# One silu for both streams, the second half first, and the loads of the opening in another order

## The chip, the cores and the metric

The program runs on one core of a Trainium2 chip. The metric is the device time of one execution in microseconds, the median over a few runs. A core has five engines with a queue of instructions each, which meet through semaphores: TensorE (PE, matrix products, with its weight loads shown as PEld), VectorE (DVE), ScalarE (ACT), GpSimd (POOL) and SyncE (SP, which here issues the DMAs). Each engine runs its queue in order, so an instruction that waits holds up everything behind it on that engine.

## The reference

The input is four images of 128 channels and 96 x 96 points. They are normalised by groups, run as a sequence in four directions (rows, rows backwards, columns, columns backwards) through one block, fused, and added to the input. The block, cut to what matters:

```python
def _scan1d(x, ...):                                # x: (16, 128, 9216), four directions of four images
    t = _grouped1x1(x, in_proj_w, in_proj_b, G)     # 4 groups, 128 -> 512 channels
    u, gate = t[:, :HID], t[:, HID:]                # HID = 256
    u = jax.nn.silu(u)
    u = depthwise_conv(u, dw_w)                     # 5 taps along the sequence
    s = _conv1x1(u, ssm_in_w)                       # 32 channels
    a = clip(DMIN + (DMAX - DMIN) * sigmoid(_conv1x1(u, ssm_delta_w, ssm_delta_b)))
    bb, cc = tanh(_conv1x1(u, ssm_b_w, ssm_b_b)), tanh(_conv1x1(u, ssm_c_w, ssm_c_b))
    hst = scan(a, bb * s)                           # h = a * h + bb * s
    u = u + _conv1x1(cc * hst + ssm_d * s, ssm_out_w)
    u = _grouped1x1(u * sigmoid(gate), mix_w, mix_b, G)
    return _conv1x1(u, out_proj_w, out_proj_b)

y = concat of the four directions, put back in place
return x + einsum('oc,bchw->bohw', fuse_w, y) + fuse_b      # the block is fed group_norm(x)
```

## The kernel before

The work of the body is cut into steps (16 lines of an image, for two directions at once) and each step into four phases `p` of the sequence, which are taken in the order `TURN = (1, 2, 3, 0)`. Position n of the sequence lies in phase n mod 4. One phase of both directions is a pair; `pair(t)` is written for the first six, `pair_on(t)` for the rest, and `tail()` ends. The two directions of a step are called the streams, `s` = 0 and 1. They lie in different partitions of the input tiles `x_in[0]` and `x_in[1]`: stream `s` in partitions 64s to 64s+63 as front rows, and the other 64 partitions hold the rows for the gate (`load_gate`).

A front is the part up to the silu. The 256 channels are two halves `j`. `in_proj(step, g, s, j, bank)` multiplies one row block of `x_in[s]` with the normalised weights `wn` in four 32 x 32 products (two passes each, so eight records in a trace). For `j` = 0 the index `g` is a group of channels and all four phases come out together; for `j` = 1 `g` is a phase. `silu` adds the bias `bnorm` and writes 385 columns of the tile `sil`; `silu_both` exists for the same over two neighbouring banks. `edges` zeroes a border column. Then the first half goes through a convolution on PE (`conv` and `conv_less`, products with the diagonal tiles `band` and `less`; each needs all four groups of the first half) and is copied to `u`. The second half goes through five taps on DVE (`taps`, lines 824 and 828). Tap k of a pair with phase p reads phase (p + k) mod 4, so the first pair (p = 1) reads the phases 1, 2, 3, 0, 1 in turn. From the second pair on the first tap is on ACT (line 826). The taps of all pairs use the same two PSUM banks, 0 and 1, so that a pair's first tap waits for the last tap of the pair before it. `proj` multiplies `u` for the scan; in the first pair it has the next step's first front between its products.

The opening is `start()`. While the first image arrives in ten pieces (`load_x`, 24 blocks), DVE takes its statistics block by block (`bn_stats`, line 330). `stats_first` then makes of them, in pieces that are released by `next(pieces)`, the group means (product with `mv`), the spreads (product with `ex`), the standard deviation, the scaled weights `wn` (line 206) and the bias `bnorm` (lines 216, 217). Between the pieces PE runs fillers, products that nobody reads. In the same place stand the fused weights: `outer(d)` multiplies the output weights with the fuse weights (line 1296, one direction `d` after the other, each emptied from PSUM by a copy), `inner` multiplies the mix weights with these (line 1304), and DVE writes them to `w_fin`, which is needed only by the last products of a pair. The order of all instructions is the order in which the program is written (a manual schedule); a wait stands wherever a tile demands it.

All loads of the opening but one are issued by SP, in the order of the program: `x`, `fuse`, `main` (the projection weights, read by line 206 and by POOL at line 398), the two front blocks, and the gates. Eight semaphores are shared among the DMAs in turn. SP therefore issues a DMA only when the one eight before it has landed.

## Time and profile before

| | us |
|---|---|
| median of 3 runs | 1717.79 |
| lowest and highest run | 1713.65, 1720.6 |
| the profiled execution | 1714.65 |
| its span on the core | 1712.9 |
| PE busy, share of the span | 1691.0, 99% |
| DVE, ACT, POOL busy | 1505.1, 1495.4, 1481.7 |
| last statistics block ends | 18.4 |
| first silu starts | 23.82 |
| last silu of the opening ends | 32.36 |

The profiled execution's own time stands beside the span of its trace; the 1.75 us between them lie around the trace. Times of the profile count from the span's start. A busy PE is not a PE at its peak, because the ends of products are modelled and overlap. In rows of the timeline an operation can be shown with its count, and in brackets stands how long its engine was idle before it and what ended that.

### The profile page before, as it was taken

The page shows a single profiled execution, that of the slowest core. Times are in us where ns is not written, and L with a number is a line of the kernel's source. Part 1 is how long each engine was busy: PE and PEld are TensorE (multiplying, and loading weights), DVE is VectorE, ACT ScalarE, POOL GpSimd, SP SyncE. Part 2 cuts the span into 40 slices and gives each one's busy share as a digit, 9 for nine tenths or more (in the row PEclk, how much of TensorE's full clock was granted, in tenths as well). Part 3 has the DMA queues.
Part 4 walks back from the last instruction along what each step waited for, and adds up shares of the span by engine and source line. Part 5 has one row for each costly group of instructions (what it writes and reads, how often), then busy time and mean ns, then how long its engine had stood idle before and what let it go on. Part 6 is the DMA issues. An engine that isn't in the chain of part 4 may idle for free.

```text
span 1712.9 us, 49914 instructions
## 1 busy us (share of the span) xinstructions
PE 1691.0 (99%) x20410; PEld 663.9 (39%) x20410; DVE 1505.1 (88%) x1506; ACT 1495.4 (87%) x2435; POOL 1481.7 (87%) x1455
## 2 busy tenths in 40 slices
PE   7999999999999999999999999999999999999998
PEld 3333333333333333333333333333333333333333
DVE  6899999888789999888888999988888888888897
ACT  4789999889889899888998898988998898988875
POOL 3689999888789999988888989999888889998887
PEclk9999999999999999999999999999999999999999
DMA  7855884468994788437897488633799538853365
GB/s 240 224 161 180 258 243 140 136 191 242 277 279 157 224 238 230 129 132 226 241 293 241 154 264 258 187 117 128 232 304 272 193 125 245 241 149 119 130 226 169
DMA packets 138949, 350.79 MB, mean 205 GB/s; under 512 B 18913, under 2 KB 85345, under 8 KB 138721
## 3 DMA queue, kind: packets, MB, share of 16 engines
q1 hardware_dynamic: 138576, 347.56, 66.7%
q8 instruction: 161, 2.64, 0.7%
q14 instruction: 68, 0.55, 0.1%
q10 hardware_dynamic: 144, 0.04, 0.0%
HBM read 191.46 MB, written 121.18 MB: 183 GB/s over the span
## 4 chain that ended last, share of the span: by engine, by line
PE 95%; DMA 3%; DVE 1%; ACT 1%; issue 0%; SPq 0%; DVEq 0%
PE psum L131 78%; PE psum L650 7%; PE psum L630 5%; PE psum L492 5%; DMA acc<-in_xr 1%; DMA sil<-sil 1%; DMA gate<-kept 1%; DVE u L711 0%; DVE bn L330 0%; DVE psum L828 0%; SPq L328 0%; PE psum L1289 0%; PE psum L1296 0%; DVE u L775 0%; PE psum L1304 0%
## 5 line engine op out<-in xcount | busy, mean ns | idle before, releaser
L828 DVE SCALAR_TENSOR_TENSOR psum<-sil,small,psum 128x768 f32<-128x768 f32 x576 | 589.1, 1023 | 52.7 <-ACT psum L826 33.8
L131 PE MATMUL psum<-u,w_fin 128*32 128x384 f32 (+1 forms) x6192 | 567.3, 485 | 3.4 <-DVE u L711 2.4
L131 PE MATMUL psum<-u,main 128*32 128x384 f32 x6144 | 535.2, 489 | 0.8 <-DVE u L775 0.4
L963 POOL TENSOR_TENSOR acc<-ys,acc 128x384 f32<-128x384 f32 x375 | 442.3, 1202 | 12.5 <-ACT ys L944 1.9
L711 DVE SCALAR_TENSOR_TENSOR u<-gate,psum 128x768 f32<-128x768 f32 x376 | 342.0, 951 | 121.1 <-PE psum L650 52.3
L131 PEld LDWEIGHTS psum<-u,w_fin 128*32 128x32 f32 x6192 | 191.2, 110 | 321.9 <-issue 233.3
L662 ACT COPY psum<-u 128x768 f32<-128x768 f32 x382 | 300.2, 798 | 12.0 <-DVE u L711 4.2
L131 PEld LDWEIGHTS psum<-u,main 128*32 128x32 f32 x6144 | 180.5, 110 | 329.3 <-issue 222.2
L131 PE MATMUL psum<-sil,band 128*32 128x384 f32 x3072 | 301.6, 488 | 0.5 <-ACT shared L516 0.5
L909 POOL TENSOR_TENSOR t<-t,t 64x384 f32<-64x384 f32 (+1 forms) x192 | 261.8, 1364 | 39.2 <-DVE t L903 22.4
L650 PE MATMUL psum<-t,main 32*128 32x384 f32 x1536 | 292.2, 521 | 0.6 <-ACT psum L662 0.5
L876 POOL TENSOR_SCALAR t<-tm 64x384 f32<-64x384 f32 x191 | 179.5, 940 | 107.7 <-ACT tm L865 95.4
L910 POOL TENSOR_TENSOR t<-t,t 64x384 f32<-64x384 f32 (+1 forms) x192 | 238.4, 1241 | 15.1
L877 POOL TENSOR_TENSOR t<-t,tm 64x384 f32<-64x384 f32 x192 | 237.5, 1237 | 15.3
L828 DVE SCALAR_TENSOR_TENSOR u<-sil,small,psum 128x768 f32<-128x768 f32 x192 | 194.9, 1015 | 6.8
L826 ACT ACTIVATE psum<-sil,small 128x768 f32<-128x768 f32 x191 | 171.7, 899 | 19.1 <-DVE u L711 16.5
L946 ACT COPY ys<-psum 128x384 f32<-128x384 f32 x288 | 137.9, 479 | 34.2 <-PE psum L131 27.7
L131 PEld LDWEIGHTS psum<-sil,band 128*32 128x32 f32 x3072 | 99.4, 110 | 150.8 <-issue 96.3
L630 PE MATMUL psum<-x_in,wn 32*128 32x384 f32 x768 | 154.2, 499 | 0.0
L492 PE MATMUL psum<-x_in,wn 32*128 32x385 f32 x704 | 143.8, 504 | 1.1 <-ACT shared L516 1.1
L650 PEld LDWEIGHTS psum<-t,main 32*128 32x128 f32 x1536 | 128.7, 184 | 33.8 <-issue 5.7
L505 ACT ACTIVATE sil<-psum,bnorm 128x385 f32<-128x385 f32 x176 | 102.1, 582 | 40.4 <-PE psum L650 20.0
(114 smaller groups left out, 1667.3 us busy)
## 6 DMA issues: line engine op xcount, KB each, us to landing
gate<-kept SPq DMA_DIRECT2D x106, 768.0 KB, 5.8
kept<-gate SPq DMA_DIRECT2D x82, 768.0 KB, 3.8
sil<-sil SPq DMA_DIRECT2D x32, 770.0 KB, 7.9
sil<-shared SPq DMA_DIRECT2D x240, 96.2 KB, 3.1
x_in<-in_xs SPq DMA_DIRECT2D x194, 96.2 KB, 3.3
out<-acc SPq DMA_DIRECT2D x46, 384.0 KB, 7.0
x_in<-in_xs SPq DMA_DIRECT2D x88, 192.5 KB, 5.8
acc<-in_xr SPq DMA_DIRECT2D x39, 384.0 KB, 6.4
```

The lines of the kernel that those rows point to most:

```text
L131: nc.tensor.matmul(o[r, : rhs.shape[-1]], lhsT, rhs, start=start, stop=stop, skip_group_check=True)
L492: nc.tensor.matmul(bank(banks[2 * j + s])[:, : N + 1], stats[units[step * UB]["b"]][0][a, s, :], x_in[s][a, q, :], start=True, stop=True,)
L630: nc.tensor.matmul(bank(to)[:, :N], stats[un["b"]][0][r, s, :], x_in[s][r, q, off : off + N], start=True, stop=True)
L650: nc.tensor.matmul(bank(ssm(bi, s) + j)[:, :N], w_so[r, bass.ts(j, P)], z[r, :], start=(bi, s) not in seeded, stop=True, skip_group_check= ...
L662: nc.scalar.copy(psum[:, ssm(bi, s) : ssm(bi, s) + 2, :N], us[bi][:, s])
L711: nc.vector.scalar_tensor_tensor(v, g, 1.0, pz, ALU.add, ALU.mult)
L828: nc.vector.scalar_tensor_tensor(us[i][:, :, 1, :] if k == K - 1 else part, src, w_tap[:, k : k + 1], part, ALU.mult, ALU.add,)
L876: nc.gpsimd.tensor_scalar(*decay(i))
L877: nc.gpsimd.tensor_mul(ta[0:64, p, :], tb[0:64, :], tm[0:64, :])
L909: engine.tensor_mul(ta[0:64, p, r], tb[64:P, r], ta[64:P, p, r])
L910: engine.tensor_add(tb[0:64, r], ta[0:64, p, r], tb[0:64, r])
L963: adder.tensor_add(part, y, part)
```

## The change

In the loads, the two front blocks and `main` come ahead of `fuse`, and only four of the eight gate loads stand here; the other four are issued after the edge stores of the opening. Between the pieces of the statistics the fillers are shorter, and the outer products are gone from there. Projections and silus go in eight fronts, the second half in turn with the first, the second half first: `(1, 1), (0, 0), (1, 2), (0, 1), (1, 3), (0, 2), (0, 3), (1, 0)` as (half, index). Each front has two neighbouring banks out of three pairs (2, 4, 6), and its silu is one operation over both streams. The outer products come after the first two bursts, through banks 0 and 1 in turn, and are all copied by DVE; the inner products follow them at once. The rows of the next step are loaded as soon as the burst is done that read their place.

```diff
     load_x([(0, 1), (1, 1), (2, 1), (3, 2), (5, 2), (7, 3), (10, 4), (14, 4), (18, 4), (22, 2)])
+    for s in range(2):
+        load_front(0, s, half(s), slice(0, R))
+    w_main = load(main, "main")
     w_out_fuse = shared()
     nc.sync.dma_start(w_out_fuse[:, 0 : 2 * HID + 4 * P], fuse)
-    w_main = load(main, "main")
-    for s in range(2):
-        load_front(0, s, half(s), slice(0, R))
-    for i in range(UB):
+    for i in range(UB // 2):
         load_gate(i)
...
-        for c, n in ((NSC - 5, 192), (NSC - 4, 192), (NSC - 3, 192), (NSC - 2, 192), (NSC - 1, 256)):
+        for c, n in ((NSC - 5, 96), (NSC - 4, 96), (NSC - 3, 96), (NSC - 2, 96), (NSC - 1, 192)):
...
         next(pieces)
-        outer(0, 0, nc.scalar.copy)
-        outer(1, 1, nc.scalar.copy)
+        filler(96)
         next(pieces)
-        outer(2, 4, nc.scalar.copy)
-        next(pieces)
-        outer(3, 5, nc.vector.tensor_copy)
-        filler(128)
+        for n in (96, 96, 96):
+            filler(n)
         for _ in pieces:
             pass
...
+        fronts = [
+            (1, TURN[0]), (0, 0), (1, TURN[1]), (0, 1), (1, TURN[2]), (0, 2), (0, 3), (1, TURN[3])
+        ]
+        def place_of(n):
+            return (2, 4, 6)[n % 3]
+        def burst(n):
+            j, g = fronts[n]
             for s in range(2):
-                in_proj(0, g, s, j, banks[j][TURN.index(g) if j else g][s])
+                in_proj(0, g, s, j, place_of(n) + s)
+            rows = None
+            if j:
+                rows = slice(g, g + 1)
+            elif g == R - 1:
+                rows = slice(0, R)
+            for s in range(2 if rows else 0):
+                load_front(1, s, slice(64 * s + 32 * j, 64 * s + 32 * j + 32), rows)
+        def silus(n):
+            j, g = fronts[n]
+            silu_both(0, g, j, place_of(n))
             edges(0, g, j, nc.vector)
-        for g in range(R):
-            burst(0, g)
-        silus(0, 0)
-        burst(1, TURN[0])
-        silus(0, 1)
-        burst(1, TURN[1])
-        silus(0, 2)
+        for n in range(2):
+            burst(n)
+        for d in range(4):
+            outer(d, d % 2, nc.vector.tensor_copy)
+        silus(0)
         inner((0, 1), 0)
         inner((2, 3), 1)
...
-        silus(0, 3)
+        burst(2)
+        silus(1)
+        burst(3)
         new_u(0)
-        burst(1, TURN[2])
-        silus(1, TURN[0])
         taps(0, (0,), nc.vector)
-        burst(1, TURN[3])
-        silus(1, TURN[1])
+        silus(2)
+        burst(4)
         taps(0, (1,))
-        conv(0, head_banks(0))
-        silus(1, TURN[2])
+        silus(3)
+        burst(5)
+        silus(4)
+        burst(6)
         taps(0, (2,))
-        silus(1, TURN[3])
+        silus(5)
+        burst(7)
+        silus(6)
+        conv(0, head_banks(0))
+        silus(7)
         conv_less(0, head_banks(0))
         taps(0, (3, 4))
         keep_lone(0)
+        for i in range(UB // 2, UB):
+            load_gate(i)
         load_lone(0)
```

The order of the instructions shows where this puts things. Numbers behind a name are those of a buffer (`x_in_70` is stream 0, `x_in_71` stream 1). First SP's queue after the pieces of `x`, before:

```order
L328 DMA acc<-in_xr 128x768
L346 DMA shared<-in_fuse 128x1024
L323 DMA main<-in_main 128x768
L298 DMA x_in_70<-in_xs 64x4x385
L298 DMA x_in_71<-in_xs 64x4x385
L316 DMA x_in_70<-in_xs 64x385
```

and now, where the fuse weights (`shared`) stand last of the four and the fronts (`x_in`, 64x4x385) first:

```order
L328 DMA acc<-in_xr 128x768
L298 DMA x_in_70<-in_xs 64x4x385
L298 DMA x_in_71<-in_xs 64x4x385
L323 DMA main<-in_main 128x768
L349 DMA shared<-in_fuse 128x1024
L316 DMA x_in_70<-in_xs 64x385
```

PE between the spreads (`ex`) and the first projections, before; the outer products are L1296:

```order
L131 MATMUL psum<-mv_217,gmean 32x1 x4
L1296 MATMUL psum<-shared 128x128 x4
L131 MATMUL psum<-ex_237,gmean 32x1 x8
L1296 MATMUL psum<-shared 128x128 x4
L1289 MATMUL psum<-acc 128x128
L131 MATMUL psum<-gm_0_239,wn_265 32x4 x4
L131 MATMUL psum<-mean_233,wn_265 32x1 x16
L131 MATMUL psum<-x_in_70,wn_265 32x385 x4
```

After these, six bursts of projections (x_in_70 and x_in_71 in turn, 12 rows) stood ahead of the inner products, L1304. The same place on PE now, down to the third burst; fillers (L1289) stand where the outer products did, and the outer and inner products stand between the second and the third burst:

```order
L131 MATMUL psum<-mv_213,gmean 32x1 x4
L1289 MATMUL psum<-acc 128x96
L131 MATMUL psum<-ex_233,gmean 32x1 x8
L1289 MATMUL psum<-acc 128x96 x3
L131 MATMUL psum<-gm_0_235,wn_256 32x4 x4
L131 MATMUL psum<-mean_229,wn_256 32x1 x16
L131 MATMUL psum<-x_in_70,wn_256 32x385 x4
L131 MATMUL psum<-x_in_71,wn_256 32x385 x4
L131 MATMUL psum<-x_in_70,wn_256 32x385 x4
L131 MATMUL psum<-x_in_71,wn_256 32x385 x4
L1296 MATMUL psum<-shared 128x128 x8
L1304 MATMUL psum<-shared 128x128 x8
```

On ACT, from the standard deviation (`std`) to the first copy of `u`, before:

```order
L1300 COPY shared<-psum 128x256 x2
L199 ACTIVATE std<-var_255 128x2
L201 ACT_TABLE_LOAD
L201 ACTIVATE first_table<-std 128x1
L1300 COPY shared<-psum 128x256
L600 ACTIVATE sil_295<-psum,bnorm_268 128x385 x16
L801 COPY u_0_1_0_378<-psum 128x2x384
```

and now, where the copies have gone to DVE and sixteen silus have become eight of twice the columns:

```order
L199 ACTIVATE std<-var_246 128x2
L201 ACT_TABLE_LOAD
L201 ACTIVATE first_table<-std 128x1
L609 ACTIVATE sil_282<-psum,bnorm_259 128x770 x8
L801 COPY u_0_1_0_350<-psum 128x2x384
```

More of the change, by code (lines that the diff above doesn't have):

```diff
@@ L1358, in start @@
                 nc.gpsimd.tensor_add(w[:, 0:e], w[:, 0:e], w[:, e : 2 * e])
-        load_rows(0, slice(0, R))
-        load_rows(1, slice(TURN[0], TURN[0] + 1))
-        silus(0, 3)
+        burst(2)
+        silus(1)
+        burst(3)
         new_u(0)
-        burst(1, TURN[2])
-        silus(1, TURN[0])
         taps(0, (0,), nc.vector)
-        burst(1, TURN[3])
-        load_rows(1, slice(TURN[1], R))
-        load_rows(1, slice(0, TURN[0]))
-        silus(1, TURN[1])
+        silus(2)
+        burst(4)
         taps(0, (1,))
+        silus(3)
+        burst(5)
+        silus(4)
+        burst(6)
+        taps(0, (2,))
+        silus(5)
+        burst(7)
+        silus(6)
         conv(0, head_banks(0))
-        silus(1, TURN[2])
-        taps(0, (2,))
-        silus(1, TURN[3])
+        silus(7)
         conv_less(0, head_banks(0))
```

8 lines of the change are left out of this document (removed).

## The prediction

> **What bounds the kernel now.** I read the page first (busy shares, the chain that ended last), then a table of stages, then the timeline of the first 45 us engine by engine, the DMA landings there, and the longest waits of the rest. The first two lines are the page's busy time of PE and its chain; the others are stages (from:to, length, busy us of PE, PEld, DVE, ACT, POOL, granted clock, DMA share, GB/s).
>
> ```profile
> PE 1691.0 (99%) x20410; PEld 663.9 (39%) x20410; DVE 1505.1 (88%) x1506; ACT 1495.4 (87%) x2435; POOL 1481.7 (87%) x1455
> PE 95%; DMA 3%; DVE 1%; ACT 1%; issue 0%; SPq 0%; DVEq 0%
> 18.44:23.82 5.38, 5.32 (x99) 4.01 (x97) 2.99 (x12) 2.69 (x6) 0.39 (x1) 1.00 1.04 216
> 23.82:36.02 12.20, 12.14 (x218) 6.46 (x222) 6.99 (x17) 9.90 (x20) 3.16 (x4) 1.00 0.55 139
> 36.02:78.60 42.58, 40.49 (x512) 13.71 (x504) 36.76 (x38) 34.96 (x62) 24.87 (x23) 1.00 0.86 245
> 78.60:1700.00 1621.40, 1617.10 (x19412) 631.03 (x19416) 1439.07 (x1403) 1442.37 (x2340) 1438.99 (x1387) 1.00 0.67 203
> ```
>
> From 78.6 us on PE is busy 1617.1 of 1621.4 us, and the change touches nothing there. So the change can only move the moment at which the rest begins: what it wins or loses before about 36 us is passed on one for one. The whole opening is 2% of the time. I take as its end the first tap of the second pair (ACT, L826 at 36.02, shown below), because from there the program is the same in both kernels.
>
> **The statistics and the weights.** Timeline of DVE and PE (start, us, engine, line, operation, out<-in, count, and the idle time before with its releaser).
>
> ```profile
> 18.44 0.81 DVE L179 BATCH_NORM_AGGREGATE mv<-bn 128x2 f32<-128x144 f32 x1
> 19.06 0.68 PE L1289 MATMUL psum<-acc 128*128 128x256 f32 x2
> 19.67 0.24 PE L131 MATMUL psum<-mv,gmean 128*32 128x1 f32 x8
> 19.84 1.16 PE L1296 MATMUL psum<-shared 128*128 128x128 f32 x8
> 20.37 0.22 DVE L188 SCALAR_TENSOR_TENSOR ex<-dev,mv 128x1 f32<-128x1 f32 x1
> 20.93 0.31 PE L131 MATMUL psum<-ex,gmean 128*32 128x1 f32 x16
> 21.93 0.48 DVE L206 TENSOR_SCALAR wn<-main,inv 128x128 f32<-128x128 f32 x2
> 22.36 0.42 DVE L1300 COPY shared<-psum 128x256 f32<-128x256 f32 x1
> 22.92 1.51 PE L131 MATMUL psum<-x_in,wn 32*32 32x385 f32 x16
> 23.35 0.17 DVE L217 TENSOR_SCALAR bnorm<-bnorm 128x2 f32<-128x2 f32 x1
> ```
>
> The aggregate ends at 18.44 + 0.81 = 19.25, but its product starts at 19.67, behind a filler of 256 columns. With shorter fillers PE keeps pace with DVE and the product can start at 19.3: 0.4 us won. `ex` ends at 20.59 and its product starts at 20.93, behind four outer products (L1296): with one 96-column filler there instead, another 0.3 us. So the scaling of the weights (`wn`, L206) could start at 21.93 - 0.7 = 21.2. ACT loses three copies of `shared`, which cost nothing where they were. But `wn` reads `main`, and `main` is now behind the front rows. SP's issues, the landing times (last number, us from issue), the first reader of `main`, and the rate of two stages of the DMA:
>
> ```profile
> 5.97 0.48 SPq L346 DMA_DIRECT2D shared<-in_fuse  x1
> 7.00 0.33 SPq L323 DMA_DIRECT2D main<-in_main  x1
> 8.42 1.98 SPq L298 DMA_DIRECT2D x_in<-in_xs  x2
> shared<-in_fuse SPq DMA_DIRECT2D x1, 512.0 KB, 12.4
> main<-in_main SPq DMA_DIRECT2D x1, 384.0 KB, 13.3
> x_in<-in_xs SPq DMA_DIRECT2D x2, 385.0 KB, 13.8
> 20.47 0.39 POOL L398 TENSOR_SCALAR main<-main 128x64 f32<-128x64 f32 x1 [9.25 <-DMA main<-in_main]
> 11.77:15.50 3.73, 3.73 (x6) 1.64 (x6) 3.73 (x8) 0.00 (x0) 0.00 (x0) 1.00 1.02 410
> 19.00:21.00 2.00, 2.00 (x28) 1.53 (x30) 0.92 (x5) 0.35 (x1) 0.39 (x1) 1.00 1.09 217
> ```
>
> Fuse lands at 5.97 + 12.4 = 18.4, main at 7.00 + 13.3 = 20.3, the second front at about 9.9 + 13.8 = 23.7. While x is loaded the engines move 410 GB/s; while the front rows are (runs of 385 elements) 217 GB/s, at the same full DMA share. Two fronts are 2 x 394 kB: 3.6 us at 217. Fuse's 524 kB at 410 are 1.3 us. Moving the fronts ahead of main and fuse behind it puts main at 20.3 + 3.6 - 1.3 = 22.6 at the latest. In the trace, though, main took 1.9 us after fuse for what 410 GB/s moves in 1.0, because faster DMA engines were already in the slow front rows; it loses that company: 21.7. The early end is 21.2, where it no longer binds. I take 21.9, near 21.7. Then `wn` starts at 21.9, as before, and the 0.7 us are not collected. (The Trainium skill, "DMA: Bandwidth & Descriptors", section Specifications, gives 512 B as the smallest transfer at line rate; by that the 1540 B runs would cost nothing extra, the fronts 1.9 us at 410, main would land at 20.9, and the sum below would be 0.7 lower. The trace does not agree: 217 against 410 GB/s.)
>
> **The silus and what now stands ahead of them on PE.** Timeline of ACT and PE; the last two rows, from later on, show how long a silu over both streams (770 columns) holds ACT.
>
> ```profile
> 23.82 0.58 ACT L600 ACTIVATE sil<-psum,bnorm 128x385 f32<-128x385 f32 x1 [0.34 <-PE psum L131]
> 24.79 5.30 ACT L600 ACTIVATE sil<-psum,bnorm 128x385 f32<-128x385 f32 x11 [0.38 <-PE psum L131]
> 27.47 2.05 PE L1304 MATMUL psum<-shared 128*128 128x128 f32 x16
> 30.36 2.00 ACT L600 ACTIVATE sil<-psum,bnorm 128x385 f32<-128x385 f32 x4 [0.28 <-PE psum L131]
> 62.94 0.91 ACT L516 ACTIVATE shared<-psum,bnorm 128x770 f32<-128x770 f32 x1
> 63.73 0.60 ACT L865 ACTIVATE tm<-psum,small 128x384 f32<-128x384 f32 x1
> ```
>
> Before, sixteen silus run nearly without a gap, every 5.30/11 = 0.48 us, to 32.36: six bursts of projections were in PSUM before PE turned to the inner products (L1304), so ACT waited only 0.28 us for those. Now a silu of both streams holds ACT 63.73 - 62.94 = 0.79 us where two took 0.96: 8 x 0.17 = 1.4 us less work. But only two bursts stand ahead of all outer and inner products.
>
> - Bursts 0 and 1: `wn` to first projection was 22.92 - 21.93 = 0.99, so 22.9; 32 records issue in about 0.8 (the row at 33.90 below lasts 1.28 with its last 0.48 of tail), so PE is free at 23.7. The second stream no longer waits for the last front (first silu pair 23.82 and 24.79 before). Fuse, now last of the four, lands around 23.3 to 24.2: I take no wait.
> - Outer products: 16 records at 0.11 (8 in 1.16 with the tail), through two banks in turn, each emptied by a DVE copy of 0.42. Outer 0 ends 24.3; copies of 0 and 1 end at 24.8 and 25.2; outer 2 runs 24.85 to 25.45, outer 3 25.3 to 25.9; their copies end at 25.9 and 26.4. The first inner products start at 25.95 and all sixteen records are issued in 1.8: 27.75.
> - ACT does silu 0 and 1 from 23.8 to 25.4 and then has nothing until burst 2 is through at 28.65 (27.75 + 0.65 + tail): 3.2 us idle, against 1.4 saved. Silus 2 to 7 follow every 0.79: silu 6 (the last of the first half) ends at 32.7, silu 7 at 33.5, 1.1 later than the last before.
>
> What hangs on silu 6, with the rows of before:
>
> ```profile
> 30.90 1.50 PE L131 MATMUL psum<-sil,band 128*32 128x384 f32 x16
> 33.90 1.28 PE L131 MATMUL psum<-x_in,wn 32*32 32x385 f32 x32
> 34.82 1.05 ACT L600 ACTIVATE sil<-psum,bnorm 128x385 f32<-128x385 f32 x2 [0.54 <-PE psum L131]
> 34.91 1.01 DVE L828 SCALAR_TENSOR_TENSOR u<-sil,small,psum 128x768 f32<-128x768 f32 x1
> 36.02 0.91 ACT L826 ACTIVATE psum<-sil,small 128x768 f32<-128x768 f32 x1 [0.15 <-DVE u L828]
> ```
>
> The first convolution needs all four groups of the first half; it started at 30.90 and the next step's projections followed 3.0 us later, their silus 0.92 after that. Now its fourth group starts at 32.85, the others a little sooner: projections at 32.85 + 3.0 - 0.2 = 35.65, silus at 36.57, and after two of them (0.93) the tap L826 at 37.5 instead of 36.02. The DVE taps, which set 36.02 before (34.91 + 1.01), are not late: the fourth waits for silu 7 at 33.5 and the last ends at 35.65. **Sum: 37.5 - 36.02 = +1.5 us.**
>
> Edits that I cost at nothing: the first four gate loads stand where they stood; the other four go to SP behind the edge stores and ahead of the load of `lone`, about 4 x 0.5 us on SP. Their readers come in the steady pairs, and `lone` is read by the third pair's add (the row below), many us later; without that cover they would cost their 2 us. The rows for the next step are loaded burst by burst; the last ones are issued around 32.5 and needed at 35.65, and if they take the median 3.8 us to land they cost 0.6.
>
> ```profile
> 47.17 1.01 DVE L775 SCALAR_TENSOR_TENSOR u<-lone,small,psum 128x768 f32<-128x768 f32 x1 [0.80 <-PE psum L131]
> ```
>
> Ends of the sum: main at 21.2 takes off 0.7, at 22.6 adds 0.7; a late fuse adds up to 0.5; a silu that holds ACT for its full 0.91 adds 4 x 0.12 = 0.5; late rows 0.6. So +0.8 to about +3.3 (not all ends at once). The profiled execution took 1714.65 (span 1712.9), so its like becomes 1716.2; the median of the runs shown lies 3.1 above it at 1717.79 and becomes **1719.3**. Under 0.5% (8.6 us) is what a measurement of this kernel can hardly tell from no change; the runs of before spread over 7 us themselves.
>
> **Rivals.**
> 1. The delay is absorbed: between 36 and 78.6 us PE is busy 40.49 of 42.58, ACT 35, DVE 37, so engines have slack there. Against: taps on DVE and the first tap on ACT wait for each other in turn in these pairs, and slack in an engine is not slack in that chain. It gives 1717.8.
> 2. The opening gets shorter: ACT's stall is covered. That needs burst 2 issued by about 25.3, 2.4 us sooner than I have it, or the convolution not to wait for silu 6. It would leave the 1.4 us of silus less small losses: 1716.6.
> 3. Slower beyond doubt: one DMA wait of the steady part multiplies. DVE waited 4.83 us for a kept gate, PE stood 2.35, and then ran at half clock for 3.4 us:
>
> ```profile
> 469.16 1.82 DVE L711 SCALAR_TENSOR_TENSOR u<-gate,psum 128x768 f32<-128x768 f32 x2 [4.83 <-DMA gate<-kept]
> 471.03 1.84 PE L131 MATMUL psum<-u,w_fin 128*32 128x384 f32 x16 [2.35 <-DVE u L711]
> 472.00:475.40 3.40, 3.40 (x29) 1.04 (x23) 3.26 (x5) 3.29 (x7) 2.89 (x4) 0.51 1.07 290
> ```
>
>    That is 2.35 + 3.4 x 0.49 = 4.0 us a time. A shift of the opening by a microsecond or two could let it come at other changes of phase; from two more on, 1.5 + 8 = 9.5 passes 8.6 us: 1727. For one more, 1723.3; if it vanishes, 1715.3. For it: its size is near the spread of the runs. Against: everything after the opening keeps its order, so DMA and readers move together.
>    (The Trainium skill, "TensorE: Matmul & The Clock Gate", Part 1, has the clock fall after an idle window of about 3.4 us; here 2.35 us of idling was enough. The longest idle stretch that I foresee in the new opening, about 1 us ahead of `wn`, is short by either.)
>
> **Chances.** Forecast (+0.8 to +3.3) 0.68; absorbed 0.12; shorter 0.08; the wait vanishes 0.05; it comes once more 0.04, twice or more 0.03. Only the last is slower by over 0.5%; none of these is faster by that much, for which I leave 0.02. So same 0.95, slower 0.03. The forecast's own range is 1718.6 to 1721.1; with cases 1 and 2 and about 2 us for the spread of a median of such runs the range is 1715.5 to 1723.
>
> **What would show it.** Right: an ACT gap of about 3 us after the second L609, ended by PE; outer and inner products between the second and third burst; main's POOL reader at about 22; L826 of the second pair near 37.5. Wrong: main landing by 21.2 or past 22.6, an ACT gap under 1 us, or L826 before 36; then the opening is shorter and the order of PE was not the limit.

## The result, and the profile after

| | before | after |
|---|---|---|
| median, us | 1715.31 (22 runs) | 1720.53 (22 runs) |
| lowest and highest run | 1711.72, 1721.86 | 1716.1, 1726.2 |
| ratio, 95% interval | | 1.0026 [1.0016, 1.0036] |
| the profiled execution, its span | 1714.65, 1712.9 | 1726.2, 1724.2 |

By the ratio the changed kernel is slower by about 4.5 us (2.7 to 6.2 by its interval). That is inside the half per cent that the prediction called "no change", but 22 runs of each tell it apart from none. Single runs of either kernel spread over 10 us, and the profiled execution of the changed kernel was its slowest run, so its total is not to be read as the typical one; the opening is.

The page of the changed kernel: PE's busy time and the chain.

```profile
PE 1695.8 (98%) x20416; PEld 664.5 (39%) x20416; DVE 1507.1 (87%) x1509; ACT 1494.6 (87%) x2424; POOL 1482.8 (86%) x1455
PE 91%; DMA 6%; DVE 1%; ACT 1%; SPq 0%; issue 0%; DVEq 0%; ACTq 0%
```

The stages of the changed kernel, cut at the same events as those of before: aggregate to first silu, first silu to the first tap of the second pair (L826), the next 42.58 us, and the rest.

```profile
19.46:25.39 5.93, 4.74 (x111) 2.86 (x110) 2.62 (x11) 1.69 (x4) 0.52 (x1) 0.87 0.77 201
25.39:40.50 15.11, 14.94 (x208) 8.26 (x210) 8.54 (x21) 8.47 (x13) 3.15 (x4) 0.94 0.39 97
40.50:83.08 42.58, 40.70 (x516) 13.96 (x508) 36.24 (x37) 34.87 (x62) 24.73 (x23) 1.00 0.87 251
83.08:1711.30 1628.22, 1618.32 (x19415) 630.50 (x19416) 1440.30 (x1403) 1443.95 (x2341) 1439.90 (x1387) 1.00 0.67 202
```

The second stage, 12.20 us before, takes 15.11. PE has fewer products in it (208 against 218) and is "busy" throughout: it runs at a granted clock of 0.94, and 0.87 in the stage ahead. The third stage is as before. The last has 9.9 us without PE where before had 4.3 in 1621.4; 7.4 of the 9.9 are the waits at three changes of phase, shown further down.

The opening, from the timeline of the changed kernel (start, us, engine, line, operation, out<-in, count, idle before and its releaser):

```profile
19.46 0.80 DVE L179 BATCH_NORM_AGGREGATE mv<-bn 128x2 f32<-128x144 f32 x1
22.93 0.48 DVE L206 TENSOR_SCALAR wn<-main,inv 128x128 f32<-128x128 f32 x2 [0.58 <-DMA main<-in_main]
22.98 0.52 POOL L398 TENSOR_SCALAR main<-main 128x64 f32<-128x64 f32 x1 [11.72 <-DMA main<-in_main]
23.71 1.70 PE L131 MATMUL psum<-x_in,wn 32*32 32x385 f32 x30
25.34 3.30 PE L1296 MATMUL psum<-shared 128*128 128x128 f32 x16
25.39 1.70 ACT L609 ACTIVATE sil<-psum,bnorm 128x770 f32<-128x770 f32 x2 [1.72 <-PE psum L131]
28.48 2.00 PE L1304 MATMUL psum<-shared 128*128 128x128 f32 x16
30.41 4.43 PE L131 MATMUL psum<-x_in,wn 32*32 32x385 f32 x96
31.41 4.87 ACT L609 ACTIVATE sil<-psum,bnorm 128x770 f32<-128x770 f32 x6 [4.33 <-PE psum L131]
34.80 2.34 PE L131 MATMUL psum<-sil,band 128*32 128x384 f32 x16
39.55 1.06 ACT L600 ACTIVATE sil<-psum,bnorm 128x385 f32<-128x385 f32 x2 [0.54 <-PE psum L131]
40.50 0.91 ACT L826 ACTIVATE psum<-sil,small 128x768 f32<-128x768 f32 x1
```

The reader is to see four things. `wn` waits 0.58 us for `main`. After two silus ACT is idle for 4.33 us, until the third burst is through PE behind all outer and inner products. The convolution starts at 34.80 and not at 30.90. L826 stands at 40.50, 4.48 later than in the profile of before. And one stage of the same profile tells why the bursts take 1.70 and the outer products 3.30 us:

```profile
23.90:27.25 3.35, 3.35 (x41) 2.08 (x32) 0.76 (x3) 1.70 (x2) 0.00 (x0) 0.50 0.21 51
```

PE ran at half clock there, which the prediction had ruled out for the opening.

### The profile page after: what moved, and what is told of

Same layout as the page of the kernel before. It is cut to its first block, busy times and chain, and to the rows that moved or that the text cites. A ratio compares the mean times of both kernels' runs of the same rounds, so it can differ in the third digit from the quotient of the medians.

```text
span 1724.2 us, 49921 instructions
## 1 busy us (share of the span) xinstructions
PE 1695.8 (98%) x20416; PEld 664.5 (39%) x20416; DVE 1507.1 (87%) x1509; ACT 1494.6 (87%) x2424; POOL 1482.8 (86%) x1455
## 4 chain that ended last, share of the span: by engine, by line
PE 91%; DMA 6%; DVE 1%; ACT 1%; SPq 0%; issue 0%; DVEq 0%; ACTq 0%
PE psum L131 74%; PE psum L650 7%; PE psum L630 5%; PE psum L492 4%; DMA gate<-kept 2%; DMA acc<-in_xr 1%; DMA main<-in_main 1%; DMA sil<-sil 1%; DMA xs<-in_xr 1%; DVE u L711 0%; DVE psum L828 0%; DMA sil<-shared 0%; SPq L523 0%; PE psum L1296 0%; ACT psum L826 0%
## 5 line engine op out<-in xcount | busy, mean ns | idle before, releaser
L909 POOL TENSOR_TENSOR t<-t,t 64x384 f32<-64x384 f32 (+1 forms) x192 | 263.4, 1372 | 39.1 <-DVE t L903 20.5
L826 ACT ACTIVATE psum<-sil,small 128x768 f32<-128x768 f32 x191 | 171.8, 899 | 25.1 <-DVE u L711 22.9
```

Source lines behind the costliest of these rows:

```text
L909: engine.tensor_mul(ta[0:64, p, r], tb[64:P, r], ta[64:P, p, r])
```

## The experiments

All times below come in three parts, which depend less on the moment at which loads land than start times do: from the aggregate (L179) to `wn` (L206), from there to the end of the opening's last silu, and from there to the second pair's L826. The moment of the aggregate itself hangs on the landing of `x`. Each number is worked out from the L179, L206, silu and L826 rows of that kernel's timeline. The ratio is to the kernel before on the same chip; "n" are the runs of the kernel.

| kernel | aggregate | to wn | to last silu | to L826 | L826 | median (n) | ratio [95%] |
|---|---|---|---|---|---|---|---|
| before | 18.44 | 3.49 | 10.43 | 3.66 | 36.02 | | |
| b2_again | 19.09 | 3.91 | 9.63 | 3.66 | 36.29 | 1718.35 (1) | |
| e5_late_gates | 19.02 | 4.09 | 9.60 | 3.66 | 36.37 | 1715.29 (12) | 1.0005 [0.9992, 1.0019] |
| e8_both | 18.78 | 3.87 | 9.92 | 3.87 | 36.44 | 1716.88 (11) | 1.0012 [0.9999, 1.0025] |
| e3_outers | 19.16 | 3.49 | 10.26 | 4.21 | 37.12 | 1715.26 (11) | 1.0003 [0.9993, 1.0013] |
| e4_inners | 19.25 | 3.50 | 11.24 | 4.34 | 38.33 | 1716.45 (12) | 1.0013 [1.0000, 1.0026] |
| after | 19.46 | 3.47 | 13.35 | 4.22 | 40.50 | 1720.53 (22) | 1.0026 [1.0016, 1.0036] |
| a2_again | 19.41 | 4.04 | 13.64 | 4.21 | 41.30 | 1723.73 (1) | |
| e1_loads | 18.99 | 3.49 | 14.31 | 4.21 | 41.00 | 1720.96 (8) | 1.0043 [1.0028, 1.0058] |
| e2_fillers | 19.80 | 4.04 | 12.22 | 4.22 | 40.28 | 1722.03 (6) | 1.0044 [1.0028, 1.0061] |
| e11_main_first | 18.53 | 2.98 | 14.20 | 4.21 | 39.92 | 1719.64 (12) | 1.0022 [1.0007, 1.0037] |
| e7_turns | 19.85 | 3.93 | 19.79 | 5.85 | 49.42 | 1728.62 (4) | 1.0086 [1.0072, 1.0099] |
| e9_turns_full | 18.83 | 3.58 | 12.30 | 7.78 | 42.49 | 1725.05 (5) | 1.0064 [1.0051, 1.0077] |
| e10_taps_apart | 19.37 | 3.60 | 14.21 | 4.38 | 41.56 | 1722.43 (12) | 1.0041 [1.0023, 1.0059] |

### e1_loads: the order of the loads alone

The changed kernel with its loads as before.

```diff
-    for s in range(2):
-        load_front(0, s, half(s), slice(0, R))
-    w_main = load(main, "main")
     w_out_fuse = shared()
     nc.sync.dma_start(w_out_fuse[:, 0 : 2 * HID + 4 * P], fuse)
+    w_main = load(main, "main")
+    for s in range(2):
+        load_front(0, s, half(s), slice(0, R))
```

> The changed kernel, with fuse, main and the fronts loaded in the order of before (fuse first). Theory A (the changed kernel lost 4.5 us in the opening as a sum of three: about 1.0 from the loads, which delay x's last pieces and main; about 1.7 from a half clock on PE at 23.9 to 27.3 us; about 1.8 from the outer and inner products ahead of the third burst): the aggregate ends at 19.25 instead of 20.26, main lands at 20.3, the scaling of the weights starts near 21.3, the second front lands at 23.7 and holds the first bursts until then; L826 of the second pair at 37.5 if the clock stays full, 39 if it drops. Rival B (the order of PE alone costs it all): L826 stays at 40.5.

L826 came at 41.00, not sooner than in the changed kernel, and the ratio is no better. From the timeline of e1_loads:

```profile
22.48 0.48 DVE L206 TENSOR_SCALAR wn<-main,inv 128x128 f32<-128x128 f32 x2
25.38 3.69 PE L1296 MATMUL psum<-shared 128*128 128x128 f32 x16
31.92 4.87 ACT L609 ACTIVATE sil<-psum,bnorm 128x770 f32<-128x770 f32 x6 [4.89 <-PE psum L131]
```

`wn` no longer waits for `main`, but ACT's gap is 4.89 us, and PE was at half clock for 6.83 us from 21.9 on, twice as long as in the first profile of the changed kernel. Theory A, with 39 at a fallen clock, missed. The old load order alone wins nothing.

### e2_fillers: the clock

The changed kernel with longer fillers behind the statistics.

```diff
-        filler(96)
+        filler(192)
         next(pieces)
-        for n in (96, 96, 96):
+        for n in (512, 384):
             filler(n)
```

> The changed kernel, with longer fillers while PE waits for main (192 columns instead of 96, and 512 and 384 instead of three of 96), so that PE stands idle for 0.3 us at most ahead of the weights. Theory A: the scaling of the weights stays at 22.9, the clock stays full from 23.9 on, the first two bursts and the products behind them take 1.7 us less, L826 at 38.8. Rival C (the half clock hides behind other waits): L826 stays within 0.4 us of 40.5.

The clock stayed full through the opening. The trace of this run holds no record of the granted clock; that it was full is read from the products. Each outer product takes 275 to 377 ns, as in e3_outers, and up to 582 in the changed kernel. From the timeline of e2_fillers:

```profile
23.84 0.56 DVE L206 TENSOR_SCALAR wn<-main,inv 128x128 f32<-128x128 f32 x2 [1.15 <-DMA main<-in_main]
25.68 2.46 PE L1296 MATMUL psum<-shared 128*128 128x128 f32 x16
28.20 2.05 PE L1304 MATMUL psum<-shared 128*128 128x128 f32 x16
30.18 4.43 PE L131 MATMUL psum<-x_in,wn 32*32 32x385 f32 x96
31.19 4.87 ACT L609 ACTIVATE sil<-psum,bnorm 128x770 f32<-128x770 f32 x6 [3.78 <-PE psum L131]
```

The outer products take 2.46 us where they took 3.30, and `wn` to the last silu takes 12.22 us, 1.1 less than in the changed kernel and 1.4 less than in its second profile. But this run's `main` landed later still, so L826 moved by only 0.22, and the total got no better (the intervals overlap). By its number this is rival C; behind `wn` it is theory A for 1.1 of its 1.7 us. Half clock is a part of the loss in the opening, and the total doesn't show it. The gap at full clock is 3.78 us: that much is the order alone.

### e3_outers and e4_inners: where outer and inner products stand

e3_outers has the loads, the fillers and the outer products of before, and keeps the rest of the change: eight fronts in turn, `silu_both`, inner products behind two bursts, four late gates. The diff is that of e3_outers to e1_loads; the line of the statistics' fillers, which is as in before, is left out of it.

```diff
-        filler(96)
+        outer(0, 0, nc.scalar.copy)
+        outer(1, 1, nc.scalar.copy)
         next(pieces)
-        for n in (96, 96, 96):
-            filler(n)
+        outer(2, 4, nc.scalar.copy)
+        next(pieces)
+        outer(3, 5, nc.vector.tensor_copy)
+        filler(128)
...
         for n in range(2):
             burst(n)
-        for d in range(4):
-            outer(d, d % 2, nc.vector.tensor_copy)
         silus(0)
         inner((0, 1), 0)
```

> Loads, fillers and outer products as before; left of the change are the eight fronts with one silu for both streams, the inner products after two bursts, and the four late gates. Theory A: as before up to the first silu; ACT stands about 1.2 us after the second silu, for the inner products alone; L826 at 36.1, within 0.5 of before. Rival D (the alternating order itself costs, through the convolution that waits for the seventh silu): 38 or more.

e4_inners puts a third burst ahead of the inner products:

```diff
-        for n in range(2):
+        for n in range(3):
             burst(n)
         silus(0)
         inner((0, 1), 0)
         inner((2, 3), 1)
...
-        burst(2)
         silus(1)
```

> As the kernel with outer products as before, but three bursts stand ahead of the inner products. Theory A: the silus run without a gap from 24.5 on and end at 31; L826 at about 34.9, 1.1 us sooner than before; over the whole 1 us faster than before, give or take the waits for kept gates at 470, 910 and 1310 us (theory E: these vary from run to run whatever the opening; theory F: they grow with the shift of the opening, and would be no larger here than before, 2.4, 0 and 0 us of idle PE). Rival D: 37 or more.

From the timeline of e3_outers:

```profile
24.92 1.70 ACT L609 ACTIVATE sil<-psum,bnorm 128x770 f32<-128x770 f32 x2 [0.73 <-PE psum L131]
25.05 2.05 PE L1304 MATMUL psum<-shared 128*128 128x128 f32 x16
28.04 4.87 ACT L609 ACTIVATE sil<-psum,bnorm 128x770 f32<-128x770 f32 x6 [1.43 <-PE psum L131]
37.12 0.91 ACT L826 ACTIVATE psum<-sil,small 128x768 f32<-128x768 f32 x1
```

With the outer products gone from between the bursts, ACT's gap falls from 4.89 (e1_loads) to 1.43 us, L826 from 41.00 to 37.12, and the ratio from 1.0043 to 1.0003, with intervals that don't meet. This is the largest step in the total that any one experiment makes, and it settles the main cause: the outer products' move out of the statistics. Two edits are in it, though, the outer products' place and the fillers that hold the clock. e2_fillers, with the outer products between the bursts at full clock, lies between the two: from `wn` to the last silu it is 14.31 in e1_loads, 12.22 in e2_fillers and 10.26 here. So 2.0 of the 4.05 us are the place and 2.1 the clock, if the load order, which differs in e2_fillers, plays no part behind `wn`. L826 at 37.12 lies between theory A (36.1, within 0.5) and rival D (38 or more).

In the run of e4_inners the second front landed at 25.16 (23.88 in e3_outers), so the first silu came late and the third burst could not show what it is worth:

```profile
25.30 1.71 PE L131 MATMUL psum<-x_in,wn 32*32 32x385 f32 x40 [0.72 <-DMA x_in<-in_xs]
26.20 2.49 ACT L609 ACTIVATE sil<-psum,bnorm 128x770 f32<-128x770 f32 x3 [1.92 <-PE psum L131]
29.91 4.08 ACT L609 ACTIVATE sil<-psum,bnorm 128x770 f32<-128x770 f32 x5 [1.21 <-PE psum L131]
```

The gap is 1.21 us instead of 1.43, and the time is no better than e3_outers. L826 at 38.33 is the number of rival D, but by the late front and not by the convolution. What a third burst is worth stays open.

### b2_again and a2_again: the same two kernels once more

> The kernel before once more, for a second profile of the same program. Theory G (the DMA of the opening varies by a microsecond from run to run, and the first profile of before was an early one): the scaling of the weights starts at 22.5 to 22.8 as in the three kernels with the old load order, not at 21.9, and L826 of the second pair at 36.5 to 37. Theory H (before is really that early, and the late gates or the other changes delayed those three): again 21.9 and 36.0. The waits for kept gates near 470, 890 and 1310 us: by theory E (they vary from run to run) another pattern than 2.4, 0, 0 us; by theory F (they follow the opening) the same.

> The changed kernel once more, for a second profile. By E another pattern of waits than 3.5, 1.3 and 2.5 us of idle PE; by F the same. ACT again stands 3.8 to 4.4 us after its second silu; whether PE runs at half clock near 24 to 27 us again decides if that is part of the change or of the run.

From the timeline of b2_again, the opening's silus and the wait for a kept gate:

```profile
24.88 7.75 ACT L600 ACTIVATE sil<-psum,bnorm 128x385 f32<-128x385 f32 x16 [0.34 <-PE psum L131]
36.29 0.91 ACT L826 ACTIVATE psum<-sil,small 128x768 f32<-128x768 f32 x1 [0.15 <-DVE u L828]
471.93 2.79 PE L131 MATMUL psum<-u,w_fin 128*32 128x384 f32 x16 [2.98 <-DVE u L711]
```

The same places from the changed kernel's first profile and from a2_again:

```profile
477.38 2.40 PE L131 MATMUL psum<-u,w_fin 128*32 128x384 f32 x16 [3.51 <-DVE u L711]
478.07 2.29 PE L131 MATMUL psum<-u,w_fin 128*32 128x384 f32 x16 [3.71 <-DVE u L711]
```

`wn` of the kernel before came at 21.93 in one run and at 23.00 in the other, L826 at 36.02 and 36.29. So a microsecond in `wn` is no finding between two profiles. The parts of the table tell more, but not under 0.8 us: over the three profiles with this opening and single silus (before, b2_again, e5_late_gates) the first goes from 3.49 to 4.09 and the second from 9.60 to 10.43, and only the third stays at 3.66. In a2_again ACT's gap is 4.45 us, and the clock is half again, for 6.83 us from 21.2 on. So both belong to the change and not to one run.

Later, PE stands idle at the three changes of phase (near 470, 900 and 1310 us) for 2.35, 0 and 0 us in the profile of before, 2.98, 0 and 1.62 in b2_again, 3.51, 1.32 and 2.54 after, 3.71, 0.71 and 1.07 in a2_again. In sum these waits vary by about 2 us within one kernel. From L826 to the end of the span it is 1676.9 us before and 1680.3 in b2_again, 1683.7 after and 1680.6 in a2_again; the four profiles with the front order of before have 1674.8 to 1680.3, the ten others 1675.9 to 1683.7. Whether the changed kernel has more of these waits is open: two profiles of each don't tell.

### e8_both and e5_late_gates: two edits on the kernel before

```diff
-            for s in range(2):
-                silu(0, g, s, j, banks[j][TURN.index(g) if j else g][s])
+            silu_both(0, g, j, banks[j][TURN.index(g) if j else g][0])
```

> The kernel before with nothing but the silus of both streams in one operation. ACT does 8 x 0.79 = 6.3 us instead of 8 x 0.96 = 7.7; but the first silu now waits for both streams, 0.6 us later, and the taps of DVE wait for the inner products as before. Theory I: the last silu ends 0.5 to 1 us sooner and L826 comes 0.3 to 1 us sooner after the second front's landing (12.3 us in the first profile of before); the total is the same within 0.1%. Rival: the whole 1.4 us arrives, 10.9 us after the front.

From the timeline of e8_both:

```profile
25.20 4.87 ACT L609 ACTIVATE sil<-psum,bnorm 128x770 f32<-128x770 f32 x6 [1.01 <-PE psum L131]
30.87 1.70 ACT L609 ACTIVATE sil<-psum,bnorm 128x770 f32<-128x770 f32 x2 [0.80 <-PE psum L131]
36.44 0.91 ACT L826 ACTIVATE psum<-sil,small 128x768 f32<-128x768 f32 x1 [0.15 <-DVE u L828]
```

Six silus of both streams take 4.87 us, 0.81 each, so the price is as forecast. But the first now waits for both streams (25.20, which is 2.55 behind `wn`, against 1.88 in b2_again), and a wait of 0.80 for PE opens further on. From `wn` to the last silu it takes 9.92 us, no less than the 9.60 to 10.43 of single silus. The saving of 1.4 us doesn't arrive anywhere; L826 waits for the DVE taps as before.

```diff
-    for i in range(UB):
+    for i in range(UB // 2):
         load_gate(i)
...
+        for i in range(UB // 2, UB):
+            load_gate(i)
         load_lone(0)
```

> The kernel before, in which only the loads of the last four gates move: from the opening to behind the opening's edge stores, where the changed kernel has them. The prediction costed this at nothing.
> Theory: nothing on the path changes; the opening's first tap (L826) within 0.5 us of the other runs of the kernel before (36.0 to 36.3), ratio 0.999 to 1.001.
> Rival 'less to move': four gates fewer in the queue let the front rows, main and fuse land sooner, so L826 comes up to 0.7 us sooner, ratio 0.9993 or less.
> Rival 'late gates': a gate comes late to its first reader in the third to eighth pair, or the load of lone behind them is late; a wait on a DMA at a gate or at lone of 0.5 us or more before 130 us, ratio over 1.0005.

Nothing moves: the three parts are those of b2_again within 0.2 us, and no wait on a load of a gate or of `lone` over 0.3 us stands between 36 and 135 us. The late gates show neither a cost nor a gain.

### e7_turns, e9_turns_full, e10_taps_apart: products in turn with bursts

If ACT starves behind thirty-two outer and inner products in one piece, they can be spread between the bursts.

```diff
-        for n in range(2):
+        for n in range(3):
             burst(n)
-        for d in range(4):
+        for d in range(2):
+            outer(d, d, nc.vector.tensor_copy)
+        silus(0)
+        burst(3)
+        silus(1)
+        for d in range(2, 4):
             outer(d, d % 2, nc.vector.tensor_copy)
-        silus(0)
+        burst(4)
+        silus(2)
         inner((0, 1), 0)
+        burst(5)
+        silus(3)
         inner((2, 3), 1)
...
-        burst(2)
-        silus(1)
-        burst(3)
         new_u(0)
-        taps(0, (0,), nc.vector)
-        silus(2)
-        burst(4)
-        taps(0, (1,))
-        silus(3)
-        burst(5)
+        taps(0, (0, 1), nc.vector)
         silus(4)
         burst(6)
```

> The changed kernel with its own loads and fillers, but the outer and inner products go in turn with the bursts: three bursts, two outer products, a burst, two outer products, a burst, half of the inner products, a burst, the other half. If it is where these products stand that costs the time (theory I), ACT never stands over 1.5 us between silus and L826 comes 2.5 to 3.5 us sooner after the scaling of the weights than in the changed kernel (17.6 us there), and the total falls to within 0.15% of before. If the loads or the alternating order cost it (rival J), L826 still comes over 16.5 us after the scaling and the total stays near 1.0026.

It was the slowest of all. A part of its timeline, and the stage from 22.10 to 42.57 us:

```profile
27.80 2.08 PE L1296 MATMUL psum<-shared 128*128 128x128 f32 x8
29.80 1.53 PE L131 MATMUL psum<-x_in,wn 32*32 32x385 f32 x16
31.44 0.90 ACT L609 ACTIVATE sil<-psum,bnorm 128x770 f32<-128x770 f32 x1 [2.56 <-PE psum L131]
22.10:42.57 20.47, 19.82 (x210) 11.18 (x210) 5.92 (x19) 7.58 (x10) 3.53 (x5) 0.50 0.17 39
```

The clock was half for 20.5 us. A pair of outer products took 2.08 us and a burst 1.53, where e9_turns_full below needs 1.16 and 0.88 at full clock, so nearly every silu waited 2.5 us. The order was not tested by this; the clock was. So the fillers of before in the statistics, and those of e2_fillers behind them, went in, and nothing else.

```diff
-        for c, n in ((NSC - 5, 96), (NSC - 4, 96), (NSC - 3, 96), (NSC - 2, 96), (NSC - 1, 192)):
+        for c, n in ((NSC - 5, 192), (NSC - 4, 192), (NSC - 3, 192), (NSC - 2, 192), (NSC - 1, 256)):
...
-        filler(96)
+        filler(192)
         next(pieces)
-        for n in (96, 96, 96):
+        for n in (512, 384):
             filler(n)
```

> The kernel with outer and inner products in turn with the bursts (e7_turns), with nothing changed but its fillers: 192 and 256 columns in the statistics, 192 and then 512 + 384 behind them, as in e2_fillers. e7_turns showed the second pair's first tap (L826) at 49.42, 25.6 us behind wn, of which 18.8 us (23.78 to 42.6) went at half clock.
> Theory 'half clock': what made the turns slow was the clock alone. At full clock the 18.8 us cost 9.4 less: L826 16.2 us behind wn, so near 39.5 with wn at 23.3; the ACT gaps fall from 2.5 us to about 1.2 each; no granted clock under 0.9 between 20 and 45 us; ratio to before 1.002 to 1.004, so about as e2_fillers and far from the 1.0086 of e7_turns.
> Rival 'turns': the order is slow by itself, PE changes to and fro with every silu waiting for a burst behind half of the products; L826 stays beyond 45, ratio 1.006 or more, with the clock full.
> Rival 'no filler holds it': the clock falls all the same, since the products and bursts in turn leave PE too little to do; half clock past 25 us, ratio 1.007 or more.

With the clock full the last silu ended 12.30 us behind `wn` instead of 19.79; that part of the theory held. L826 came at 42.49 and not at 39.5, though. From the timeline of e9_turns_full:

```profile
33.01 1.70 ACT L609 ACTIVATE sil<-psum,bnorm 128x770 f32<-128x770 f32 x2 [1.02 <-PE psum L131]
33.89 2.15 DVE L828 SCALAR_TENSOR_TENSOR psum<-sil,small,psum 128x768 f32<-128x768 f32 x2
36.14 3.00 PE L131 MATMUL psum<-sil,band 128*32 128x384 f32 x12 [2.44 <-DVE sil L553]
```

Two taps stood on DVE ahead of the edges (L553) that the convolution needs: PE waited 2.44 us, and the clock fell at 35.7, within that wait. So this run doesn't tell what the order in turn is worth: two taps had been put together. The next kernel takes them apart:

```diff
         silus(2)
+        new_u(0)
+        taps(0, (0,), nc.vector)
         inner((0, 1), 0)
         burst(5)
         silus(3)
+        taps(0, (1,))
         inner((2, 3), 1)
...
-        new_u(0)
-        taps(0, (0, 1), nc.vector)
```

> e9_turns_full with one thing mended: its first two taps of the second pair on DVE (the L824 and L828 rows at 32.83 and 33.89) stood in one piece ahead of the edges of silus 4 to 7, so the first convolution waited 2.44 us for an edge (L553 at 36.03), PE stood still and ran the next 3.41 us at half clock. Here tap 0 stands behind silu 2 and tap 1 behind silu 3, as in the changed kernel.
> Theory 'my own taps': last silu ends at 33.9 as in e9_turns_full, the edges follow at once, the convolution's last part starts about 34.1, L826 at 38.2 to 38.9 (the changed kernel has 40.50, the kernel before 36.02); no half clock between 20 and 45 us; ratio to before 1.001 to 1.0035.
> Rival 'turns': products between the bursts cost in themselves; L826 stays beyond 40.5 and the ratio beyond 1.004, the wait ahead of the convolution only changes its name.
> Rival 'the rest': L826 comes to 39 or less, and the time stays 1.005 or more above before, by waits for kept gates and half clock after 70 us; then the opening isn't what the time hangs on here.

The wait ahead of the convolution is down to 0.33 us, but another came. From the timeline of e10_taps_apart:

```profile
30.37 1.16 PE L1304 MATMUL psum<-shared 128*128 128x128 f32 x8 [0.77 <-DVE psum L824]
33.38 1.16 PE L1304 MATMUL psum<-shared 128*128 128x128 f32 x8 [1.04 <-DVE psum L828]
```

The taps and the inner products share PSUM banks 0 and 1, so with a tap ahead of it each inner product waits for DVE. L826 at 41.56 and the ratio of 1.0041 are the numbers of the rival "turns", but 1.8 us of them are this wait. The order in turn gave no gain in any of the three kernels. What it would be worth with banks of its own is open.

### e11_main_first: main ahead of the fronts

e2_fillers with `main` loaded ahead of the front rows, and `fuse` last as in the change.

```diff
+    w_main = load(main, "main")
     for s in range(2):
         load_front(0, s, half(s), slice(0, R))
-    w_main = load(main, "main")
```

> e2_fillers (the changed kernel with longer fillers) with main loaded ahead of the two front rows, fuse last as before. In all five profiles with the fronts ahead, wn waits for main (0.58, 1.07, 1.15, 1.04 and 0.41 us); in the seven with main ahead it never did.
> Theory 'main late': wn no longer waits for a load; wn follows the aggregate by 3.3 us (4.04 in e2_fillers); main lands at 20.5 to 21.5; the fronts land near 24, the first silus lose a part of it again, so L826 comes 0 to 0.8 us after 16.4 + wn, 39.0 to 40.0; ratio 1.002 to 1.004 (e2_fillers 1.0044).
> Rival 'all of it': the fronts are not late, L826 below 39.0, ratio under 1.002.
> Rival 'fronts late': the front rows, now behind main, land past 24.5 and hold the first bursts; L826 at 40.3 or later, ratio 1.004 or more.

From the timeline of e11_main_first:

```profile
21.51 0.48 DVE L206 TENSOR_SCALAR wn<-main,inv 128x128 f32<-128x128 f32 x2
25.32 2.45 PE L1296 MATMUL psum<-shared 128*128 128x128 f32 x16 [1.16 <-DMA shared<-in_fuse]
30.84 4.87 ACT L609 ACTIVATE sil<-psum,bnorm 128x770 f32<-128x770 f32 x6 [4.98 <-PE psum L131]
```

`wn` follows the aggregate by 2.98 us, the shortest of all. The short fillers of the statistics, which it keeps, may give these 0.5 us; e1_loads has the same ones and no wait for `main`, and needs 3.49, because there PE reached the product of `mv` only 1.47 us behind the aggregate's start (1.01 here). L826 at 39.92 and the ratio of 1.0022 lie where the theory "main late" put them, but by luck: L826 comes 18.4 us behind `wn` and not 16.4 to 17.2, and the fronts weren't late. PE waited 1.16 us for `fuse`, and ACT's gap became 4.98. What is won ahead of `wn` is lost behind it: about 1.5 us up to the outer products, most of it the wait for the last of the four loads, and 0.5 because PE comes to its first product behind `wn` only after the long fillers (0.93 us against 0.42 in e2_fillers). The time is that of the changed kernel within the intervals.

No kernel here beats the one before; e3_outers, e5_late_gates and e8_both can't be told from it.

## Why the prediction was right or wrong, point by point

- **The opening carries the change one for one: right for the changed kernel.** L826 is 4.3 us later than its mean over the three profiles with the opening of before (36.02, 36.29, 36.37), 5.1 in a2_again, and the ratio makes 4.5 of the whole (the medians differ by 5.2). The rival "absorbed" fell, and so did "shorter". In e2_fillers and e9_turns_full the ratio makes more, 7.5 and 11.0 us (4.8 and 8.7 at the lower ends), where L826 of their one profile is 4.1 and 6.3 later; what the rest is stays open.
- **The mechanism: right.** The gap on ACT stands behind the second silu of both streams, PE ends it, and outer and inner products lie in it. e3_outers shows that most of it goes with the outer products (4.89 to 1.43 us).
- **Statistics and `main`: right in the net, the landing outside its ends.** `main` was read at 22.98, above the upper end of 22.6. But the aggregate too started 1.02 later than in the profile of before, and `wn` stands 3.47 behind it, where the forecast had 3.46. In the six profiles with the fronts ahead of it, `wn` waited for `main` 0.41 to 1.15 us, so what the short fillers may gain was not collected, as written. The step left out that `x` itself came later: the aggregate starts at 19.45 on average in these six and at 18.91 in the eight with `main` ahead of the fronts. The ranges (18.83 to 19.85, 18.44 to 19.25) overlap, and why is open. That the front rows are slow for the length of their runs, as the prediction has it, is not shown either. A front also fills only 64 partitions, and packets of 1540 B took a median of 121 ns among themselves (before, 19 to 21 us), but 66 ns beside those of the image (after, 12.0 to 15.5 us). (The Trainium skill, "DMA: Bandwidth & Descriptors", Specifications, by whose line rate `main` would have landed at 20.9, does not fit: the reader at 22.98 is 2.1 later, of which the later aggregate makes 1.0.)
- **The clock: the step that failed.** The prediction held the idle stretch ahead of `wn` for "short by either" the trace's 2.35 us or a window of 3.4. The clock fell in both profiles of the changed kernel, for 3.41 and 6.83 us, though in the 8 us ahead of the fall no wait of PE was longer than 0.75 us. The sum has no term for it. It cost 1.1 to 1.4 us between `wn` and the last silu (13.35 and 13.64 against 12.22 in e2_fillers).
- **Outer and inner products: mis-sized.** "All issued" 4.05 us after PE is free was 5.07 in the changed kernel and 4.50 at full clock (25.68 to 30.18 in e2_fillers). That made the 3.2 us of idle ACT 4.33. The two bursts ahead took until 25.34, 2.41 behind `wn` where 1.8 was forecast; at full clock they need 1.84. So of these 1.6 us 1.1 are the clock, and 0.45 are the products' own size. `fuse` landed at 24.5, a little past the forecast's 24.2, and PE did not wait for it, as forecast.
- **From the last silu on: nearly right.** 4.0 forecast, 4.22 measured, 3.66 before. The convolution does wait for the seventh silu. The alternate order has 4.21 or more here in every kernel, e3_outers too, so 0.55 us more than before; e8_both, with silus of both streams in the old order, has 3.87.
- **The silus' saving: the price right, the gain wrong.** 0.81 us each against 0.79 forecast. e8_both shows that on the old order the gain doesn't reach the path.
- **Late gates and rows burst by burst, costed at nothing: right** for the gates (e5_late_gates). For the rows, the silus at 39.55 wait 0.54 us for PE as they did before, which shows none late.
- **The sum:** +1.5 forecast with ends at +0.8 and +3.3; about +4.5 measured, outside the ends. Between the 37.5 forecast for L826 and the 40.50 in the profile lie 1.0 for the later aggregate, 0.6 for the bursts, 1.0 for the products, 0.1 for the silus and 0.2 behind them. That 1719.3 lies only 1.2 below the measured 1720.53 is partly luck: the three runs of before had a median 2.5 above that of 22, which made up for most of the missing rise.
- **The wait for kept gates (rival 3): neither shown nor excluded.** It came at three changes of phase in the changed kernel's profiles, but also at two in the second profile of before.

## What to carry to other kernels

Work that seems free because it stands between dependent steps is paid when it is moved into the stretch where another engine waits for the same queue: ask which queue the moved instructions join, and who is behind them. Ask also what they did where they stood: here the outer products' place was filled with shorter products, and the clock fell. When two profiles of one kernel differ by a microsecond in when loads land, compare intervals between events of the same chain, and not start times. And a saving per operation (here about 0.16 us on each silu) counts only if the operation's inputs are ready; making one operation wait for both streams took it back.

## What the runs showed of the hardware

The clock fell in the opening of all four profiles with only 96-column fillers behind the products of `mv` and `ex` (after, a2_again, e1_loads, e7_turns), at 21.2 to 23.9 us, and in the opening of none of the ten with longer fillers or outer products there, but for e9_turns_full, where PE had waited 2.44 us. The stage before the fall in e1_loads:

```profile
18.50:21.90 3.40, 3.02 (x44) 2.60 (x44) 2.04 (x7) 0.00 (x0) 0.39 (x1) 1.00 1.08 216
```

PE counts as busy for 3.02 of 3.40 us there, with products of 192 columns or fewer. In e7_turns (row above) it counts as busy for 19.82 of 20.47 us and stays at half clock. So busy time as the records give it doesn't say whether the clock holds. The half-clock stretches lasted 3.41, 6.83 and 20.48 us, that is 1, 2 and 6 times 3.41. (The Trainium skill, "TensorE: Matmul & The Clock Gate", Part 1, gives a free-running window of 3413 ns, which these lengths agree with. It has the clock fall after at least one idle window and rise after one busy one; the rows of e1_loads and e7_turns agree with neither. What decides it no run here shows.)
